# First cross attention of a Perceiver block: scores by key kept in SBUF, their maxima taken by key and turned

## The chip, the cores and the metric

The kernel runs on one core of one Trainium2 chip. The engines of a core work side by side, each through its own queue in order: TensorE (PE, matrix products; its weight loads are shown as PEld), VectorE (DVE), ScalarE (ACT), GpSimd (POOL) and SyncE (SP, which here only issues transfers). They meet through semaphores. Products land in PSUM, the other operands lie in SBUF. The metric is the device time of one execution in microseconds, the median of several runs.

## The reference, cut to what matters

The whole computation is a chain of twelve blocks (attention, feed-forward and expert layers) on `x` of shape (16, 64, 256), four of which attend to a context of shape (16, 1601, 256). The change touches the first of them alone. Its weights are `w_q, w_k, w_v, w_o` (256 x 256). As the kernel computes it, with 16 heads of 16 columns, for each batch `b`:

```python
h = layernorm(x)
q, k, v = h @ w_q, ctx @ w_k, ctx @ w_v           # heads of 16 columns
s = einsum('qd,kd->qk', q[head], k[head])         # 64 x 1601 for each of 16 heads
s = where((s == 0) & (key <= query), finfo.min, s)   # zeros at and below the diagonal do not count
p = softmax(s / 4)
x = x + concat(p @ v[head]) @ w_o
```

All of it is in fp32. The softmax subtracts the true maximum over the 1601 keys for each query and head.

## The kernel before

The keys of a batch are cut into 13 chunks of 128 (the last has 65 valid rows), so there are 16 x 13 = 208 chunks. The 256 columns are two groups `g` of 128; a group holds four blocks of 32 rows, and a block holds two heads. `x.qb` keeps each query twice, once with the columns of the even heads and once with those of the odd ones (zeros elsewhere, `own2`), so that one product over 32 rows gives two heads side by side in 128 columns (2 heads x 64 queries). Four such products, one for each block, run beside each other on the array; so do four products with 32 weight columns each (`columns`).

`stream` (L2507) writes TensorE's whole order out by hand: with `self.pinned` every matmul issued by `mm` and `tr` keeps the order of the program. One step `k` handles two chunks:

1. `weights` (L335) makes the scores of the chunk pair of the next step in the four-bank PSUM tile `sc` (tag `w`, one buffer): `scores_by_key` (L2447) gives keys on the partitions; then products of `minus` and `x.rows` subtract the maxima inside PSUM, in bf16 parts, and products of `x.z` with `never` put a huge negative value where a score was zero at or below the diagonal. ScalarE's exponential (L361) reads the tile into `e`.
2. `project` (L2515) makes the next piece of keys (`kT`) or values (`v`) of a later batch in a PSUM tile `pk` (tag `bk`, two buffers), which ScalarE copies out (L286). Each batch has 13 pieces: six of keys, one with the last chunk of both, six of values.
3. `values` (L2553) multiplies the exponentials by the values into `acc`; GpSimd adds the exponentials up over the chunks into `tot` (L2551), from which `finish_heads` (L2418) makes the sums with products of ones.
4. The jobs of `extra` (L395) make the maxima for a batch ahead of its weights: `maxima` (L288) makes all scores of a batch a second time, by query, in the same PSUM tile `w`; VectorE reduces 2048 columns at a time (L299); `last_maxima` (L301) handles the last chunk, joins the parts and splits the result into three bf16 parts; `max_rows` (L324) turns them into rows.

`load` (L267) fetches a batch's context with two transfers on SP's queue and makes `qb` on GpSimd; for the second batch it also calls `gate_biases` (L1139), which prepares a bias of a later stage. `out` (L398) makes the output product of two batches (128 rows), adds it to `x` and, at the last rows, begins the next stage (`start`, `norm`, `turned`). The pool `weights` (`w8`, L114, three buffers of 8 KB a partition) belongs to no stage: in this one the next stage's large weights are already fetched into it (L118). `awake` (L2632) issues products whose result nobody reads.

Of the kernel before, what the change touches and what calls it, by code (L numbers as in the profile page):

```python
# [20 lines left out]
P = 128  # L21
# [43 lines left out]
class Sections:  # L65
# [157 lines left out]
    def l0_xattn(self):  # L223
# [6 lines left out]
        with ExitStack() as ctx:  # L230
            sb = ctx.enter_context(tc.tile_pool(name="l0x", bufs=1, reuse_waits="tile"))
            sb2 = ctx.enter_context(tc.tile_pool(name="l0x2", bufs=2, reuse_waits="tile"))
            ps = ctx.enter_context(tc.tile_pool(name="l0x_ps", bufs=2, space=PSUM, reuse_waits="tile"))
            wq = self.w2(d["L0_xattn_w_q"], "wq")
# [4 lines left out]
            xln = sb2.tile([P, NT, D], F32, tag="e", name="xln", bufs=3)  # L239
            xT = sb.tile([P, KC, T], F32, tag="xT", name="xT")  # L240
            qT = sb.tile([P, KC, T], F32, tag="qT", name="qT")
            identb = sb.tile([P, P], BF16, tag="identb", name="identb")
            nc.vector.tensor_copy(identb, self.ident)
            minus = sb.tile([P, P], BF16, tag="minus", name="minus")
            nc.gpsimd.memset(minus, -1.0)
            never = sb.tile([P, P], BF16, tag="never", name="never")
            nc.vector.tensor_scalar(never, self.ident, NEVER, None, ALU.mult)
            parts = sb.tile([P, 4, 32], BF16, tag="parts", name="parts")
            nc.gpsimd.memset(parts, 0.0)
# [9 lines left out]
            own = self.c("own2")  # L259
            tril = self.c("tril2").unsqueeze(1).to_broadcast([P, 4, S])  # L260
            ones = self.c("ones")[:, :32]

            def quad():

                return ps.tile([P, 4, 512], F32, tag="w", name="sc", bufs=1)

            def load(b):  # L267
                if b == 1:
                    self.gate_biases(sb2)
                x = Streamed(b)  # L270
# [3 lines left out]
                x.v = sb2.tile([P, NCH, D], F32, tag="v", name="v")  # L274

                x.qb = sb2.tile([P, 2, 2, S], F32, tag="qb", name="qb", bufs=3)
                nc.gpsimd.tensor_tensor(
# [3 lines left out]
                x.m4 = sb2.tile([P, 2, 4, 4], F32, tag="m4", name="m4")  # L281
                x.z = sb2.tile([P, 2, 4, S], BF16, tag="z", name="z", bufs=3)
                return x

            def copy(out, in_):
                nc.scalar.copy(out, in_)  # L286

            def maxima(x, g, i):  # L288


                pm = quad()
                for r in range(4):
                    o = slice(32 * r, 32 * r + 32)
                    self.mm(
                        pm[:, r, :], x.qb[o, g].rearrange("p h s -> p (h s)"), x.kT[i][o, g, :512], start=True, stop=True)
                if i == 0:
                    nc.vector.scalar_tensor_tensor(x.z[:, g], pm[:, :, :S], 0.0, tril, ALU.is_equal, ALU.mult)
                    nc.vector.scalar_tensor_tensor(pm[:, :, :S], x.z[:, g], NEVER, pm[:, :, :S], ALU.mult, ALU.add)
                nc.vector.tensor_reduce(x.m4[:, g, :, i], pm, AX.X, ALU.max)  # L299

            def last_maxima(x):  # L301


                w = SK - 1536
                pm = quad()
                for g in range(2):
                    for r in range(4):
                        o = slice(32 * r, 32 * r + 32)
                        self.mm(
                            pm[:, r, g * P : g * P + w], x.qb[o, g].rearrange("p h s -> p (h s)"),  # L310
                            x.kT[2][o, g, 512 : 512 + w], start=(g == 0), stop=True, skip_group_check=True,
                        )
                nc.vector.tensor_reduce(
# [4 lines left out]
                for s in range(3):  # L318
                    to = parts[:, :, 2 * s : 2 * s + 2]
                    nc.vector.tensor_copy(to, m)  # L320
                    if s < 2:
                        nc.vector.tensor_tensor(m, m, to, ALU.subtract)
# [12 lines left out]
            def weights(pair):  # L335

                pm = quad()
                if pair[0][0].b == pair[0][1] == 0:
                    self.awake(ps, 2, "acc")
# [2669 lines left out]
```

## Time and profile before

| what | value |
|---|---|
| median of 3 runs | 3684.61 us (3680.84 to 3687.91) |
| the profiled execution, its own time | 3680.2 us |
| its span, first to last instruction | 3678.4 us |
| mean granted clock of TensorE | 0.984 |
| first product of the keys of this stage (L2622, tile `pk`) | 20.6 us |
| last output of its heads (L2436) | begins at 851.9 us |
| ScalarE copying keys and values (L286), 128x512 | 585 to 586 ns |
| GpSimd adding exponentials (L2551), 128x1024 | 2363 ns between 100 and 700 us |

A row of a group reads: line, engine, operation, output <- inputs, shapes, count | busy time, mean ns of one | idle time of the engine just before, and what ended it. In a timeline a row reads: start, length, engine, line, operation, names, shapes, count, and in brackets the idle time before. One line stands for all products that helpers issue: L2622 is inside `mm`, so products are told apart by their tiles. A matmul in fp32 leaves two records, one in bf16 leaves one.

### The profile page before, as it was taken

How to read it: one execution, taken by the hardware profiler on the slowest of the kernel's cores; microseconds unless marked ns; L12 is line 12 of the kernel's file. 1: busy time of each engine (PE TensorE's matmuls, PEld its weight loads, DVE VectorE, ACT ScalarE, POOL GpSimd, SP SyncE). 2: the span in 40 equal slices, each digit the busy share in tenths (PEclk: the TensorE clock that was granted, in tenths of full speed). 3: DMA queues.
4: the chain of work that ended last, by engine and by line, in shares of the span. 5: the costliest groups of instructions: out<-in, count | busy, mean ns of one | idle time of the engine just before them, and what ended most of it. 6: DMA issues, size and time to landing. Idle time of an engine off the chain costs nothing.

```text
span 3678.4 us, 87682 instructions
## 1 busy us (share of the span) xinstructions
PE 3444.5 (94%) x39417; PEld 2061.5 (56%) x39432; DVE 1974.8 (54%) x3645; ACT 1457.2 (40%) x2093; POOL 1290.7 (35%) x784
## 2 busy tenths in 40 slices
PE   9999999998999989999987988999999889999997
PEld 3555555454665665555555666556666555555554
DVE  5344333446555646656656555577777765333446
ACT  2333333343444424444433443466666612111124
POOL 1555555562101123333322100577777630000002
PEclk9999999999999989999999999999999999999999
DMA  4111001101333355342101000211111004111550
GB/s 148 39 39 39 29 31 39 39 8 55 98 91 99 121 168 168 121 149 105 45 27 41 1 6 22 94 58 40 53 45 40 9 5 177 40 38 33 242 220 13
DMA packets 108135, 260.82 MB, mean 71 GB/s; under 512 B 9609, under 2 KB 76172, under 8 KB 105456
## 3 DMA queue, kind: packets, MB, share of 16 engines
q1 hardware_dynamic: 99040, 223.14, 17.1%
q10 hardware_dynamic: 6912, 27.27, 2.4%
q8 instruction: 309, 5.06, 0.6%
q0 software_dynamic: 1808, 4.80, 0.4%
q14 instruction: 66, 0.54, 0.0%
HBM read 248.85 MB, written 6.33 MB: 69 GB/s over the span
## 4 chain that ended last, share of the span: by engine, by line
PE 73%; DVE 14%; ACT 8%; issue 3%; DMA 1%; POOL 0%; SPq 0%; ACTq 0%; DVEq 0%; POOLq 0%
PE sc L2622 15%; PE pk L2622 14%; PE lin L2622 6%; ACT e L361 5%; PE lin_t L2622 5%; PE acc L2622 5%; PE pu L2622 4%; PE gate L2169 3%; PE up L2169 3%; PE lin L216 3%; PE pc L1789 3%; PE prz L2622 2%; DVE m L299 2%; PE gelu_t L1703 2%; PE turn L2640 1%
## 5 line engine op out<-in xcount | busy, mean ns | idle before, releaser
L2551 POOL TENSOR_TENSOR tot<-tot,e 128x1024 f32<-128x1024 f32 (+1 forms) x340 | 807.1, 2374 | 349.6 <-ACT e L361 237.3
L299 DVE TENSOR_REDUCE m<-sc 128x4 f32<-128x2048 f32 x96 | 220.1, 2293 | 267.6 <-PE sc L2622 266.5
L1932 DVE SCALAR_TENSOR_TENSOR e<-sc,row_L_xattn_nbias,free 128x2048 f32<-128x2048 f32 x104 | 244.3, 2349 | 104.9 <-PE sc L2622 101.2
L1934 ACT ACTIVATE e<-e 128x2048 f32<-128x2048 f32 x104 | 198.6, 1910 | 232.5 <-DVE e L1932 232.5
L2622 PE MATMUL sc<-qb,kT 32*128 32x128 f32 x6656 | 245.0, 284 | 47.6 <-DVE e L1932 17.8
L361 ACT ACTIVATE e<-sc 128x2048 f32<-128x2048 f32 x104 | 195.2, 1877 | 224.2 <-PE sc L2622 222.6
L2622 PEld LDWEIGHTS sc<-qb,kT 32*128 32x128 f32 x6656 | 206.1, 187 | 92.8 <-issue 24.8
L2622 PEld LDWEIGHTS acc<-e,v 128*32 128x32 f32 x6656 | 189.1, 110 | 75.9 <-issue 50.6
L2622 PE MATMUL acc<-e,v 128*32 128x128 f32 x6656 | 221.4, 273 | 5.1 <-ACT e L1935 5.1
L2622 PE MATMUL pk<-cT,wk 128*32 128x512 f32 (+1 forms) x2048 | 205.4, 519 | 4.5 <-ACT kT L286 4.5
L2622 PE MATMUL pk<-wv,cT 128*32 128x256 f32 x3328 | 203.4, 382 | 0.0
L1935 ACT ACTIVATE e<-e 128x2048 f32<-128x2048 f32 x104 | 198.8, 1912 | 3.2
L2622 PE MATMUL pk<-wkv,cT 128*32 128x256 f32 x3328 | 193.5, 381 | 0.0
L2622 PE MATMUL pk<-cT,wkv 128*32 128x512 f32 (+1 forms) x2048 | 192.5, 515 | 0.0
L2622 PE MATMUL sc<-kT,qb 32*128 32x512 f32 (+2 forms) x1536 | 140.2, 460 | 23.3 <-ACT e L361 18.6
L2622 PEld LDWEIGHTS pk<-wv,cT 128*32 128x32 f32 x3328 | 97.7, 110 | 112.3 <-issue 57.4
L2173 ACT ACTIVATE g<-gate 128x512 f32<-128x512 f32 x68 | 40.6, 597 | 293.3 <-PE gate L2169 293.3
L1789 PE MATMUL pc<-ew,eh 128*128 128x256 f32 x640 | 156.7, 388 | 0.0
L1322 POOL TENSOR_TENSOR e<-e,mx 128x512 f32<-128x512 f32 x96 | 81.8, 883 | 193.1 <-DVE mx L1321 193.1
L2174 DVE TENSOR_TENSOR hT<-up,g 128x512 f32<-128x512 f32 x68 | 47.0, 691 | 182.3 <-PE up L2169 178.6
L2210 POOL TENSOR_TENSOR x<-x,row_L_xattn_bv 128x1024 f32<-128x1024 f32 x2 | 4.7, 2346 | 396.6 <-DVE xln L158 396.6
L2622 PE MATMUL pu<-cn,e 128*64 128x257 f32 (+1 forms) x1248 | 141.6, 382 | 1.6 <-POOL e L1332 1.5
(544 smaller groups left out, 6468.0 us busy)
## 6 DMA issues: line engine op xcount, KB each, us to landing
cT<-in_ctx_t SPq DMA_DIRECT2D x128, 832.0 KB, 6.2
cn<-in_ctx_n SPq DMA_DIRECT2D x32, 1664.0 KB, 12.0
piece<-in_ctx_n ACTq DMA_DIRECT2D x32, 640.0 KB, 4.0
w<-in_L_attn_W SPq DMA_DIRECT2D x8, 1024.0 KB, 6.5
piece<-in_ctx_n ACTq DMA_DIRECT2D x16, 384.0 KB, 3.7
w<-in_L_ffn_W SPq DMA_DIRECT2D x16, 256.0 KB, 2.9
down<-in_L_ffn_w_down SPq DMA_DIRECT2D x16, 256.0 KB, 2.8
gate<-in_L_ffn_w_gate SPq DMA_DIRECT2D x16, 256.0 KB, 2.8
```

The lines of the kernel that those rows point to most:

```text
L216: nc.tensor.matmul(pm, xT[:, k, t * P : (t + 1) * P], w[:, k, :], start=(k == 0), stop=(k == kc - 1))
L299: nc.vector.tensor_reduce(x.m4[:, g, :, i], pm, AX.X, ALU.max)
L361: nc.scalar.activation(e, pm, AF.Exp, scale=0.25)
L1322: pin(nc.gpsimd.tensor_tensor(p.e, p.e, p.mx.unsqueeze(2).to_broadcast(p.shape), ALU.subtract))
L1703: nc.tensor.matmul(pm, w[:, c, lo : lo + m], cT[:, c, :], start=(c == 0), stop=(c == nk - 1))
L1789: nc.tensor.matmul(pc[:, n, j, :], s.eh[i][:, c, tok], ew2[:, c, cols], start=False, stop=(c == 3))
L1932: nc.vector.scalar_tensor_tensor(e16, pm16, nb, free[:, at : at + P].unsqueeze(1).to_broadcast([P, 16, P]), ALU.add, ALU.mult)
L1934: nc.scalar.activation(e, e, AF.Relu)
L1935: nc.scalar.activation(e, e, AF.Square)
L2169: nc.tensor.matmul(pm[-1], w[:, k, n * P : (n + 1) * P], xT[:, k, tok], start=(k == 0), stop=(k == KC - 1))
L2551: nc.gpsimd.tensor_tensor(tot[:w], x.first if c == 1 else tot[:w], e[:w], ALU.add)
L2622: ins = self.nc.tensor.matmul(*args, **kw)
```

## The change

The products by query are gone. A unit is now one batch and one group `g` (32 units); the order runs over quads, four chunks of 13 x 32 = 416, so 104 quads and five more rounds to drain (`LAG`).

- A quad's scores are made once, by key, in the PSUM tile `w` (still one buffer of four banks). `hide` puts in the masked zeros on VectorE for the first chunk of a unit. ScalarE copies the four banks to an SBUF tile `raw`; VectorE takes the running maximum of each chunk into `top` of the unit (128 keys' places x 4 blocks x 128).
- After a unit's last chunk `turn_maxima` turns `top` by products with the identity, VectorE reduces over the places, `spread_maxima` turns the result back so that every partition has the row of maxima, and ScalarE copies it to `mx`.
- `lower` subtracts `mx` from the raw scores on GpSimd (on VectorE for the last four quads); ScalarE then makes the exponential in place, in SBUF.
- The values are kept with a column of ones for each pair of heads (16 + 1 columns a head, interleaved by a strided copy on VectorE), so that the products of the values also give the sums; each head has its own product of 64 columns. `finish` joins the halves, moves the sums with products of `pair_sum`, and scales.
- Seven buffers hold the raw scores: four of this stage, three in `w8`. The copies of the keys stay on ScalarE, those of the values go to VectorE. VectorE, ScalarE and GpSimd are written in order too (`Written`).
- A further constant, `heads`, is fetched on SP's queue, and `gate_biases` is called before the loop, ahead of the first `load`.

```diff
+            V, A, G = (Written(tc, e) for e in (nc.vector, nc.scalar, nc.gpsimd))
...
+            heads = sb.tile([P, 3, P], F32, tag="heads", name="heads")
+            nc.sync.dma_start(heads, d["heads"].rearrange("p (k n) -> p k n", n=P))
...
+            vs = [sb.tile([P, NCH, H // 2, 2, 17], F32, tag=f"v{i}", name="v") for i in range(2)]
+            for v in vs:
+                nc.gpsimd.memset(v, 1.0)
...
+            self.gate_biases(
+                [sb2.tile([32, 2, 4 * D], F32, tag="raw", name="bias_raw", bufs=4)[:, i] for i in range(2)],
+                sb2.tile([32, 4 * D], BF16, tag="kT", name="part", bufs=5))
+
+            UNITS, LAG, LEAD = 2 * B, 5, 4
+            Q = UNITS * NCH // 4
...
+            order = [(keys, 0, 0), "v", (keys, 0, 1), "v", (keys, 0, 2), (last_keys,), "v", (keys, 1, 0), "v",
+                     (keys, 1, 1), "v", (keys, 1, 2), "v"]
+            LATE = 2
...
+            def scores(q):
+
+                pm = ps.tile([P, 4, 4, P], F32, tag="w", name="sc", bufs=1)
+                for i in range(4):
+                    b, g, c = of(4 * q + i)
+                    x = xs[b]
+                    kT, at = (x.kT[g, c // 4], c % 4 * P) if c < 12 else (x.last[:, g], 0)
                     for r in range(4):
                         o = slice(32 * r, 32 * r + 32)
                         self.mm(
+                            pm[:, r, i, :], kT[o, at : at + P], x.qb[o, g].rearrange("p h s -> p (h s)"),
+                            start=(i == 0), stop=True, skip_group_check=True)
+                return pm
+
+            def hide(q, pm):
+
+                for i in range(4):
+                    if (4 * q + i) % NCH == 0:
+                        shape = [S, 4, P]
+                        of = pm[:S, :, i, :]
+                        z = sb2.tile(shape, BF16, tag="z", name="z")
+                        V.scalar_tensor_tensor(
+                            z, of, 0.0, upto[:S].unsqueeze(1).to_broadcast(shape), ALU.is_equal, ALU.mult)
+                        V.scalar_tensor_tensor(of, z, NEVER, of, ALU.mult, ALU.add)
+
+            def maxima(q, pm):
+
+                for i in range(4):
+                    n = 4 * q + i
+                    u, c = divmod(n, NCH)
+                    if c == 0:
+                        us[u] = Streamed(u)
+                        us[u].top = sb2.tile([P, 4, P], F32, tag="top", name="top")
+                        V.tensor_copy(us[u].top, pm[:, :, i, :])
+                        continue
+                    w = min(P, SK - c * P)
+                    top = us[u].top[:w]
+                    V.tensor_tensor(top, top, pm[:w, :, i, :], ALU.max)
...
+            def keep_values(x, pm, cs):
+                V.tensor_copy(
+                    x.v[:, cs[0] : cs[0] + len(cs), :, :, :16],
+                    pm[:, : len(cs) * D].rearrange("p (j a h e) -> p j a h e", h=2, e=16, a=H // 2))
...
+            def turn_maxima(u):
+
+                pt = ps.tile([P, 4, P], F32, tag="bk", name="mt")
                 for r in range(4):
+                    for j in range(4):
+                        o = slice(32 * j, 32 * j + 32)
+                        self.mm(pt[o, r, :], us[u].top[:, r, o], self.ident, start=(r == 0), stop=True, skip_group_check=True)
+                us[u].m = sb2.tile([P, 4], F32, tag="m", name="m")
+                V.tensor_reduce(us[u].m, pt, AX.X, ALU.max)
+
+            def spread_maxima(u):
+
+                pt = ps.tile([P, 4, P], F32, tag="bk", name="mx")
+                for r in range(4):
+                    self.tr(pt[:, r, :], us[u].m[:, r : r + 1].to_broadcast([P, P]), self.ident)
+                us[u].mx = sb2.tile([P, 4, P], F32, tag="mx", name="mx", bufs=3)
+                us[u].pt = pt
+
+            def lower(q, E):
...
+                    E.tensor_tensor(part, part, us[u].mx.unsqueeze(2).to_broadcast([P, 4, to - n, P]), ALU.subtract)
...
+            def values(q):
...
+                    pairs = xs[b].v.rearrange("p c a h e -> p c a (h e)")
+                    for h in range(2):
+                        for j in range(4):
+                            self.mm(
+                                u.acc[32 * j : 32 * j + 32, h * S : (h + 1) * S], pairs[:w, c, 4 * g + j, h : h + 32],
+                                e[:w, j, i, h * S : (h + 1) * S], start=(c == 0 and h == 0), stop=(c == NCH - 1),
+                                skip_group_check=True)
...
+            def take(u):
+                us[u].sums = sb2.tile([P, P], F32, tag="sums", name="sums")
+                A.copy(us[u].sums, us[u].acc[:, :P])
+
+            def finish(u):
+                x = us.pop(u)
+                acc = x.acc
+                for h in range(2):
+                    for j in range(4):
+                        o = slice(32 * j, 32 * j + 32)
+                        self.mm(acc[o, 2 * S : 3 * S], pair_sum[:, h, o], x.sums[:, h * S : (h + 1) * S],
+                                start=(h == 0), stop=(h == 1), skip_group_check=True)
+                both = sb2.tile([P, S], F32, tag="both", name="both")
+                V.tensor_scalar(both, acc[:, :S], own[:, 0:1], None, ALU.mult)
+                V.scalar_tensor_tensor(both, acc[:, S : 2 * S], own[:, 1:2], both, ALU.mult, ALU.add)
+                V.reciprocal(acc[:, 3 * S : 4 * S], acc[:, 2 * S : 3 * S])
+                b, g = divmod(u, 2)
+                V.tensor_tensor(hT[:, g, b * S : (b + 1) * S], both, acc[:, 3 * S : 4 * S], ALU.mult)
...
+            for q in range(-(LEAD // 2), Q + LAG):
+                new, old = 0 <= q < Q, 0 <= q - LAG < Q
+                for u in ends(q - 1):
+                    A.copy(us[u].mx, us[u].pt)
+                closed = ends(q - 1 - LAG)
+                for u in closed:
+                    take(u)
+                if 0 <= q - LAG + 1 < Q:
+                    lower(q - LAG + 1, G if q < Q else V)
+                if new:
+                    pm = scores(q)
+                if old:
+                    A.activation(raws[q - LAG], raws[q - LAG], AF.Exp, scale=0.25)
+                if new:
+                    hide(q, pm)
+                    if q % 7 < 3:
+                        raws[q] = self.wp.tile([P, 4, 512], F32, tag="w8", name="raw", bufs=3)
+                    else:
+                        raws[q] = sb2.tile([P, 4, 512], F32, tag="raw", name="raw", bufs=4)
+                    raws[q] = raws[q].rearrange("p r (i n) -> p r i n", n=P)
+                    A.copy(raws[q], pm)
+                    maxima(q, pm)
+                piece(2 * q + LEAD)
+                for u in closed:
+                    finish(u)
+                piece(2 * q + LEAD + 1)
+                for u in ends(q):
+                    turn_maxima(u)
+                if 0 <= q - Q + 7 < NT - 1:
+                    out(q - Q + 7)
+                if old:
+                    values(q - LAG)
+                for u in ends(q):
+                    spread_maxima(u)
+            take(UNITS - 1)
+            finish(UNITS - 1)
+            self.awake(ps, 3, "bk")
+            out(NT - 1)
```

## The prediction

> **What bounds the kernel now.** I read the page first (busy shares, the chain that ended last), then the groups by shape from 100 to 700 us, where the first cross attention runs undisturbed, then its timeline, then rows of other stages that have the shapes of the new instructions.
>
> ```profile
> PE 3444.5 (94%) x39417; PEld 2061.5 (56%) x39432; DVE 1974.8 (54%) x3645; ACT 1457.2 (40%) x2093; POOL 1290.7 (35%) x784
> PE 73%; DVE 14%; ACT 8%; issue 3%; DMA 1%; POOL 0%; SPq 0%; ACTq 0%; DVEq 0%; POOLq 0%
> ```
>
> TensorE is busy 94% of the span and 73% of the chain. In the stage, by group:
>
> ```profile
> L299 DVE TENSOR_REDUCE m<-sc 128x4 f32<-128x2048 f32 x72 | 165.1, 2293 | 204.7 <-PE sc L2622 203.9
> L361 ACT ACTIVATE e<-sc 128x2048 f32<-128x2048 f32 x77 | 144.5, 1877 | 172.5 <-PE sc L2622 172.5
> L2622 PE MATMUL sc<-kT,qb 32*128 32x512 f32 x572 | 81.6, 639 | 15.3 <-ACT e L361 15.3
> L2622 PE MATMUL sc<-rows,minus 32*128 32x512 bf16 x284 | 28.7, 374 | 0.0
> ```
>
> 72 reductions, six a batch, are 12 batches. VectorE and ScalarE wait for TensorE (204.7 and 172.5 us); it hardly waits for them. The timeline gives durations and the pace:
>
> ```profile
> 205.50 0.18 DVE L317 TENSOR_REDUCE m<-m 128x8 f32<-128x32 f32 x1
> 205.52 1.17 PE L2622 MATMUL sc<-qb,kT 32*128 32x128 f32 x32 [0.82 <-DVE m L313]
> 206.51 0.39 PE L2622 MATMUL sc<-rows,minus 32*128 32x512 bf16 x4
> 206.84 1.92 PE L2622 MATMUL pk<-cT,wk 128*32 128x512 f32 x16
> ...
> 711.11 0.19 DVE L317 TENSOR_REDUCE m<-m 128x8 f32<-128x32 f32 x1
> ```
>
> Ten batches lie between the two L317: 50.56 us each, 101.1 for two. The stage's first product starts at 20.6 us and its last output ends at 852.1: 831 us, of which 16 batches at this pace are 809 and 22 lie at the ends.
>
> **TensorE's share of the change.** Removed per batch, busy time of the groups over 12: the maxima's products 81.6 and 8.1 us (6.8 + 0.7), `rows` 2.6, `never` 0.6, the sums from `tot` 0.6, the turned parts 0.2, and 3 us of waits: about 14.5. Added per batch: two turns of the maxima (32 records each, like a 32-record `acc` burst, 1.06 us), two spreads (8 transposing records, 1.04 us by the row of L182), 0.45 for the head sums: 4.6. The values take twice as many matmuls of half the width; a burst of this very shape stands in a later stage:
>
> ```profile
> 3001.16 1.10 PE L2622 MATMUL acc<-qp,kv 128*32 128x64 f32 x64
> ```
>
> 64 records (an fp32 matmul leaves two) are one quad (four chunks of 128 keys), 0.9 us until the next can start: per batch 5.9 us against 7.0 before. If TensorE still set the pace, some 10 us a batch, 145 to 175 us, would go.
>
> **What takes its place.** A quad's scores now leave PSUM twice: ScalarE copies the tile (L361's shape, 1.85 us) and VectorE takes maxima of it, four operations of 128x512. PSUM tile `w` has one buffer, so the next quad's scores, next in TensorE's written order, wait for both. Do both read at once? L1796 and L1797 tell: ScalarE and VectorE read the same PSUM tile into different tiles, and no data passes between them, yet:
>
> ```profile
> L1797 DVE TENSOR_SCALAR rb<-pc x24: 680/690/693, 1994.5 to 2259.3; 128x512 f32<-128x512 f32 x24
> ...
>   ACT sp L1796: 32.7, 10
> ```
>
> VectorE waited ten times, 32.7 us, for ScalarE's reading to end. In the first transposes it is the other way round: ScalarE's reading starts 0.03 us after VectorE's ends, four times of four. So I take the readings as one after the other, copy before maxima, as written; each maxima operation touches all four banks of the copy, so none can start early. The Trainium skill speaks on both sides. PSUM — Partial Sum Buffer, section Specifications (TRN2), gives ScalarE and VectorE full bandwidth in parallel, as long as banks do not collide; by that the time would be the first rival's below. Its section PSUM bank collisions raise a hardware error counts two engines reading one bank and the same 32 partitions as such a collision; by that it is my forecast.
>
> A maxima operation reads one PSUM and one SBUF operand: 691 ns by L2174 (128x512, same operands). A dependent VectorE operation starts 0.03 after the one before. Loop of a plain quad: scores 1.17, hand-over 0.07, copy 1.85, 0.03, maxima 4 x 0.69 + 3 x 0.03 = 2.87, back to TensorE 0.06: **6.05 us**. TensorE's own work in it: 0.99 + two projections of 1.74 + 0.90 = 5.37. Loop, not TensorE, sets the pace.
>
> Thirteen quads are two batches and hold four unit ends (a unit is one batch and 128 of its 256 columns):
> - Five plain: 30.6 (one is 6.4, `take` and the exponential being late).
> - Three after a unit's end: ScalarE copies the spread maxima (0.59) and does the exponential (1.91) before its copy, which starts at 2.5 instead of 1.2: 7.3 each, 22.0.
> - One of these with `hide` first (64x512, 0.69 and 0.70): 7.5.
> - Four ends. The turn needs the finished maxima and a `bk` bank. With `hide` the copy ends at 4.6, maxima at 7.4; if the first projection was of values, its bank is read out by VectorE after them, 8.1. Turn 1.06, reduction 0.69, spread 0.87 to TensorE's next: 11.1 with a late start of VectorE, twice. With keys first the turn starts at 6.8, but 1.2 of finishing stands before the reduction: 10.6. Without `hide` 9.6. Sum 42.4.
>
> Total 102.5 against 101.1: +1.4 per two batches, **+11 us** over eight. Ends: 3.5 of first projections; first maxima wait some 6 for the ten gate-bias operations (VectorE until 31 us; they stood before the first maxima already); after the last quad subtractions on VectorE (2048 elements, 2.29 by L1802's 1223 ns for 1024), exponentials and finish, 16; three for the last output products. 29 against 22: **+7**.
>
> **The clock.** In the two longest ends TensorE stands idle 3.6 us before the turn. Windows (length, then busy time of PE, PEld, DVE, ACT, POOL with counts, granted clock, DMA share, GB/s) show what such a pause does:
>
> ```profile
> 34.00:38.00 4.00, 3.56 (x20) 0.91 (x24) 2.30 (x2) 0.00 (x0) 0.00 (x0) 0.62 0.26 84
> ...
> 2921.00:2925.00 4.00, 4.00 (x40) 2.95 (x44) 2.66 (x4) 3.70 (x2) 0.19 (x3) 0.50 0.00 0
> ```
>
> The first follows 2.98 us without a matmul, the second 4.14: the granted clock is 0.62 and 0.50 over four us, and the 32 score records at 2920.9 take 2.09 instead of 1.17. 0.62 is 3 us at half speed, so 1.5 us lost. For 16 such ends that is 24 us; nothing, if all of it falls into the loop's slack. Turn, values and spread (2.8 us) directly follow the pause and lie on the path, so I take three quarters: **+18**.
>
> **Work off the path.** GpSimd subtracts 2048 elements a quad: 2.30 ns each by L2551, 4.7 us, against 7.9 a quad on average; by L1322 (883 ns for 512) 3.5. It stays hidden up to 7.9. It loses the sums (`tot`). Its two fills with ones (3536 columns; 0.95 us for 1024) end by 10 us, before its first use at 19.8. ScalarE: 1.85 + 1.91 + 0.9 a quad, hidden but for the cases above. SP's queue gets the `heads` load (196 KB) and the gate biases ahead of the first context: some 1.6 us, while that landed long before its use at 20.6. Three `w8` buffers hold scores until the stage's end, so two 1 MB weight loads move from 23.7 us to there; first use is 58 us after it (910.2), landing 6.5: covered; uncovered 7 to 13 us.
>
> **Sum.** Profiled execution 3680.2 (span 3678.4 and 1.8 around it) + 11 + 7 + 18 = 3716; the median shown is 4.4 above that execution: **3721**. The same walk laid over the old order gives 98.1 for two batches where the trace has 101.1, 3% short; as much here is +25.
>
> **Rivals.** One, faster: both engines do read at once. The loop is 1.17 + 0.07 + 2.87 + 0.06 = 4.2, under TensorE's 5.37; ends wait 1 to 2 us; two batches take 82.4, so 8 x 18.7 = 150 us go, the ends give back 5: **3540**. It decides if the first maxima start within 0.2 us of the scores' end. For it: nothing passes between the two readers; against it, the 32.7 us above. Chance 0.11. Two, no slower: the walk is 3% too long (25) because late exponentials and read-outs overlap better than a strict order says, and the clock stays up (18): **3678**. For it: the pauses of 0.8 us before scores in 205.5 to 711.1 us left the granted clock at 1.00; against it, the walk was short, not long, on the old order. 0.24, of which 0.14 faster and 0.10 the same. Three: GpSimd's subtraction and VectorE's maxima exclude each other: 4.7 + 2.9 and 1.3 of other VectorE work are 8.9 a quad, 104 x 1.0 more than 7.9: **3825**. For it: L2436 (two SBUF inputs) takes 1232 ns under GpSimd's sums and 293 without; against it, L428 (one input in PSUM, like the maxima) took 418 with GpSimd busy. 0.05. My forecast has 0.60.
>
> **From these.** The range goes down to 3655 (the second rival without the 7 at the ends and another 2% of the walk, 16) and up to 3765 (25 as on the old order, 6 to the clock's full 24, 13 for uncovered weights). A measurement of this kernel tells some 0.2%, 7 us, from no change. Faster 0.14 + 0.11 = 0.25, same 0.10, slower 0.60 + 0.05.
>
> **What would show it.** Maxima starting 0.03 us after the raw copy, TensorE waiting for VectorE's maxima before scores (0.6 us in plain quads) and before turns (2 to 4 us); 51 us between the ends of batches; GpSimd without waits on VectorE; values near 0.9 a quad; long records after the turns' waits. Maxima beginning with the copy prove me wrong at once; an even pace of 41 us a batch too.

## The result and the profile after

The changed kernel takes 3715.17 us (median of 3711.39 to 3716.35), the kernel before 3684.51 beside it: a ratio of 1.0082, interval 1.0064 to 1.0099. It is slower, by 30.7 us; 3721 was forecast. The profiled execution is one of 3715.3 us, its span 3713.5 against 3678.4, the mean granted clock 0.972 against 0.984.

The page's busy times and its chain by engine:

```profile
PE 3370.3 (91%) x42270; PEld 2086.1 (56%) x42270; DVE 2103.7 (57%) x4048; ACT 1608.6 (43%) x2149; POOL 1315.9 (35%) x721
PE 65%; DVE 21%; ACT 9%; issue 4%; POOL 0%; DMA 0%; another core or an unknown queue 0%; SPq 0%; ACTq 0%; DVEq 0%; POOLq 0%
```

TensorE's busy time fell by 74 us (3444.5 to 3370.3), and yet the span grew by 35: TensorE now waits. VectorE's share of the chain rose from 14% to 21%. The groups between 100 and 750 us name the partners:

```profile
L59 POOL TENSOR_TENSOR raw<-raw,mx 128x2048 f32<-128x2048 f32 x65 | 296.6, 4594 | 89.2 <-ACT mx L59 89.2
L59 DVE TENSOR_TENSOR top<-top,sc 128x512 f32<-128x512 f32 x285 | 195.8, 687 | 241.5 <-ACT raw L59 234.1
...
L59 ACT COPY raw<-sc 128x2048 f32<-128x2048 f32 x84 | 156.6, 1864 | 83.0 <-PE sc L2739 45.4 <-DVE sc L59 36.8
...
L2739 PE MATMUL sc<-qb,kT 32*128 32x128 f32 x2488 | 95.6, 284 | 54.7 <-DVE top L59 53.2 <-ACT raw L59 1.5
```

Read upwards from the last row: TensorE's scores wait for VectorE's maxima (53.2 us), the maxima wait for ScalarE's copy (234.1), the copy for the scores or for `hide`: a ring of three. GpSimd's subtraction, with 4.59 us the longest operation here, waits only for `mx`; nobody's row names it as the releaser. (L2739 is now the line in `mm`, L59 the one in `Written`.)

The timeline of two quads, the first after a unit's end, the second plain:

```profile
460.03 1.17 PE L2739 MATMUL sc<-qb,kT 32*128 32x128 f32 x32
...
460.62 1.92 ACT L59 ACTIVATE raw<-raw 128x2048 f32<-128x2048 f32 x1
...
462.43 1.86 ACT L59 COPY raw<-sc 128x2048 f32<-128x2048 f32 x1
...
464.32 2.85 DVE L59 TENSOR_TENSOR top<-top,sc 128x512 f32<-128x512 f32 x4 [4.93 <-ACT raw L59]
...
467.32 1.17 PE L2739 MATMUL sc<-qb,kT 32*128 32x128 f32 x32 [1.64 <-DVE top L59]
...
468.61 1.87 ACT L59 COPY raw<-sc 128x2048 f32<-128x2048 f32 x1 [0.79 <-PE sc L2739]
...
470.50 2.85 DVE L59 TENSOR_TENSOR top<-top,sc 128x512 f32<-128x512 f32 x4 [2.73 <-ACT raw L59]
```

In the plain quad the copy starts 1.29 us after the scores did, the maxima 0.02 after the copy's end, and 0.16 after the maxima the next scores start, at 473.51: 6.19 us. In the one before, `mx` and the exponential hold the copy up until 462.43, and the quad takes 7.29.

Where do the 30.7 us lie? From the first scores, at 25.9 us in both kernels, 91 quads (14 batches) take 705.1 us; at the old pace of 50.56 a batch they took 707.8. The loop itself is a draw, 2.7 us better. The last 13 quads and what follows, up to the next stage's first `lin_t` (869.2 us in the kernel before, 894.7 now), take 163.7 us against 135.5: +28.2. The stage as a whole gives +25.5. The rest of the span, +9 to 10 in the profiled execution, comes up in stages whose instructions did not change; it is looked at with the experiments.

### The profile page after: what moved, and what is told of

The parts are those of the page before. It is cut to its first block, busy times and chain, and to the rows that moved or that the text cites. A ratio compares the mean times of both kernels' runs of the same rounds, so it can differ in the third digit from the quotient of the medians.

```text
span 3713.5 us, 93831 instructions
## 1 busy us (share of the span) xinstructions
PE 3370.3 (91%) x42270; PEld 2086.1 (56%) x42270; DVE 2103.7 (57%) x4048; ACT 1608.6 (43%) x2149; POOL 1315.9 (35%) x721
## 4 chain that ended last, share of the span: by engine, by line
PE 65%; DVE 21%; ACT 9%; issue 4%; POOL 0%; DMA 0%; another core or an unknown queue 0%; SPq 0%; ACTq 0%; DVEq 0%; POOLq 0%
PE pk L2739 11%; PE sc L2739 10%; DVE top L59 7%; PE lin L2739 7%; ACT raw L59 5%; PE lin_t L2739 5%; PE pu L2739 4%; PE acc L2739 3%; PE gate L2286 3%; PE up L2286 3%; PE lin L216 3%; PE pc L1906 3%; PE prz L2739 2%; PE turn L2757 2%; PE gelu_t L1820 2%
## 5 line engine op out<-in xcount | busy, mean ns | idle before, releaser
L59 POOL TENSOR_TENSOR raw<-raw,mx 128x2048 f32<-128x2048 f32 (+3 forms) x123 | 460.0, 3772 | 342.4 <-ACT mx L59 342.4
L2668 POOL TENSOR_TENSOR tot<-tot,e 128x1024 f32<-128x1024 f32 (+1 forms) x170 | 405.7, 2387 | 105.8 <-ACT e L2052 78.9
L59 DVE TENSOR_TENSOR top<-top,sc 128x512 f32<-128x512 f32 (+1 forms) x384 | 263.8, 687 | 314.8 <-ACT raw L59 304.9
L2739 PE MATMUL sc<-qb,kT 32*128 32x128 f32 x6400 | 244.1, 286 | 81.1 <-DVE top L59 63.5
L2739 PEld LDWEIGHTS sc<-qb,kT 32*128 32x128 f32 x6400 | 205.1, 189 | 120.4 <-ACT raw L59 40.8
L59 ACT COPY raw<-sc 128x2048 f32<-128x2048 f32 x104 | 193.8, 1864 | 116.6 <-PE sc L2739 62.1
L2739 PE MATMUL pk<-wv,cT 128*32 128x256 f32 x3328 | 212.0, 394 | 0.1
L2739 PE MATMUL pk<-cT,wk 128*32 128x512 f32 (+1 forms) x2048 | 202.1, 516 | 0.0
L59 ACT ACTIVATE raw<-raw 128x2048 f32<-128x2048 f32 x104 | 199.3, 1918 | 1.7 <-POOL raw L59 0.9
L2739 PE MATMUL pk<-wkv,cT 128*32 128x256 f32 x3328 | 193.5, 381 | 0.0
L2739 PE MATMUL pk<-cT,wkv 128*32 128x512 f32 (+1 forms) x2048 | 192.5, 514 | 0.0
L2739 PEld LDWEIGHTS pk<-wv,cT 128*32 128x32 f32 x3328 | 104.8, 113 | 83.2 <-issue 27.7
L2739 PE MATMUL sc<-cT,qT 128*64 128x512 f32 (+1 forms) x768 | 142.1, 520 | 4.7 <-ACT scs L1419 4.2
L2739 PE MATMUL pu<-cn,e 128*64 128x257 f32 (+1 forms) x1248 | 141.2, 381 | 2.0 <-POOL e L1449 2.0
```

Of the source, the lines that this page charges most:

```text
L59: ins = getattr(self.engine, name)(*args, **kw)
L2668: nc.gpsimd.tensor_tensor(tot[:w], x.first if c == 1 else tot[:w], e[:w], ALU.add)
L2739: ins = self.nc.tensor.matmul(*args, **kw)
```

## The experiments

The theory under test: **the two readings of the one PSUM tile stand in a row, copy before maxima, and this ring sets the loop; what is late at its end (the turn, the next copy) makes the long quads**. Against it: TensorE's own work or clock, VectorE and GpSimd holding each other up, GpSimd's subtraction, the stage's end. "13 quads" is a cycle of two batches, 99.7 us in the changed kernel's undisturbed cycles.

**x1: maxima from the copy in SBUF.**

```diff
-                    maxima(q, pm)
+                    maxima(q, raws[q])
```

> VectorE takes the maxima from ScalarE's copy in SBUF, not from the PSUM tile; result unchanged. Theory (the two readings of the one PSUM tile stand in a row and set the pace): the tile is free when the copy ends, 1.17 + 0.07 + 1.85 + 0.06 = 3.2 us after the scores began, under TensorE's own 5.4, so plain quads fall from 6.18 to about 5.4, quads after a unit's end from 7.3 to about 5.8, ends stay near 9.7 (the turn still waits for the maxima); 13 quads 88 instead of 99.7, the kernel about 3625. Rival A (with both operands in SBUF, VectorE's maxima and GpSimd's subtraction hold each other up): maxima of 1.2 us each instead of 0.69, subtractions well over 4.7, ends 2 us longer, 13 quads 96 to 110, the kernel 3690 to 3800. Rival B (TensorE's own work or its clock sets the pace): 13 quads stay at 99.7, the kernel at 3715.

Measured: 3991.95 us, ratio to before 1.0844 (1.0822 to 1.0865); 13 quads 139. The PSUM tile is free early, as meant: quads come down to 5.6 where VectorE runs freely. But VectorE does not. Two views of one place in its timeline, VectorE's and GpSimd's:

```profile
294.28 2.80 DVE L59 COPY top<-raw 128x512 f32<-128x512 f32 x1 [2.01 <-ACT raw L59]
297.12 4.92 DVE L59 TENSOR_TENSOR top<-top,raw 128x512 f32<-128x512 f32 x1
...
292.22 9.27 POOL L59 TENSOR_TENSOR raw<-raw,mx 128x2048 f32<-128x2048 f32 x2
```

A maxima operation of 0.69 us takes 4.92 while GpSimd subtracts; 84 of 416 operations on `top` took over 1.5 us, the longest 11.9. So rival A is real, and far stronger than the 1.2 us expected from a row of the trace before. The Trainium skill has the rule (SBUF — State Buffer, section Who interferes with whom): a VectorE operation with two inputs in SBUF and a GpSimd operation that reads SBUF exclude each other, for a whole instruction at a time. This run agrees, with 4.92 for 0.69; in the changed kernel, where one of the inputs lies in PSUM, 285 maxima average 687 ns beside the same subtractions.

**x8: x1 without the subtraction**, to tell that from slow operands.

```diff
-                    E.tensor_tensor(part, part, us[u].mx.unsqueeze(2).to_broadcast([P, 4, to - n, P]), ALU.subtract)
```

> x1 (maxima from the copy in SBUF) with the subtraction of the maxima left out as in x4, so that GpSimd is all but idle. Theory (x1's maxima of 1.5 us mean, up to 2.9, come from VectorE and GpSimd holding each other up where both have all operands in SBUF): maxima fall to 0.7 us or less, GpSimd's few other operations stay, plain quads about 5.4, ends about 9; 13 quads 83 to 90 instead of x1's 139, the kernel about 3610. Rival (a VectorE operation with two operands in SBUF is slow by itself, or the copy's late end sets the pace): maxima stay above 1.2 us, 13 quads above 120, the kernel above 3850.

Measured: 3655.13 us, ratio 0.9927 (0.9901 to 0.9954); 13 quads 93 to 98, more than expected, since the turn at a unit's end still waits for copy and maxima (55.2 us for VectorE's maxima between 100 and 690 us). The group of the maxima from 100 to 690 us:

```profile
L59 DVE TENSOR_TENSOR top<-top,raw 128x512 f32<-128x512 f32 x275 | 190.3, 692 | 197.4 <-ACT raw L59 190.4
```

692 ns with GpSimd quiet, 1496 in x1. The mutual exclusion is shown. With the maxima in SBUF most plain quads are 5.58 to 5.80, near the 5.4 that was estimated for TensorE's own work: that they were 6.19 was due to the PSUM tile.

**x2 and x5: the tile in halves.** Both split the scores into two PSUM tiles of two banks. They differ in the order in which four readings are written. x2:

```diff
-                    A.copy(raws[q], pm)
-                    maxima(q, pm)
+                    A.copy(raws[q][:, :2], pm[0])
+                    A.copy(raws[q][:, 2:], pm[1])
+                    maxima(q, pm[1], slice(2, 4))
+                    maxima(q, pm[0], slice(0, 2))
```

> The scores of a quad lie in two PSUM tiles of two banks; ScalarE copies half one, then half two, VectorE takes the maxima of half two first, then of half one; result unchanged, VectorE has 8 operations of 128x256 a quad for 4 of 128x512. Theory (readings in a row): the engines read different halves at once; both are read 1.17 + 0.07 + about 3.1 = 4.3 us after the scores began, under TensorE's 5.4; plain quads 5.4 instead of 6.18, the turn at an end hardly waits (8.3 instead of 9.7), after an end about 6.3 instead of 7.3; 13 quads about 86 instead of 99.7, the kernel about 3605. If copy and maxima of different banks do not run at once either, or TensorE's own work sets the pace: 13 quads stay at 99 to 103, the kernel at 3715 or above.

Measured: 3799.07 us, ratio 1.0316 (1.0299 to 1.0334); 13 quads 112.6. The expectation failed, and the timeline says how:

```profile
345.96 1.93 ACT L59 COPY raw<-sc 128x1024 f32<-128x1024 f32 x2 [2.34 <-PE sc L2743]
...
347.92 3.48 DVE L59 TENSOR_TENSOR top<-top,sc 128x256 f32<-128x256 f32 x8 [2.48 <-ACT raw L59]
```

VectorE starts after both copies, since its first four operations read the half that is copied second, and the copy of that half is written ahead of them. The reading written first goes first; separate banks alone gain nothing. x5 exchanges two lines:

```diff
                     A.copy(raws[q][:, :2], pm[0])
-                    A.copy(raws[q][:, 2:], pm[1])
                     maxima(q, pm[1], slice(2, 4))
+                    A.copy(raws[q][:, 2:], pm[1])
                     maxima(q, pm[0], slice(0, 2))
```

(`hide` does half one first as well.)

> As x2_halves, with two lines exchanged: the order written is copy of half one, maxima of half two, copy of half two, maxima of half one (x2 had both copies written ahead of both maxima, and its VectorE began only after the second copy, although no bank was shared). Result unchanged. Theory (a reading of a PSUM tile waits for the reading of the same tile written before it by the other engine, and for nothing else): maxima of half two start within 0.2 us of the scores' end, beside the copy of half one; both halves are read 1.17 + 0.07 + 8 x 0.435 = 4.7 us after the scores began, under TensorE's 5.4; plain quads 5.4 instead of after's 6.18, after an end about 5.9 instead of 7.3, ends 8.3 or (with hide) 10; 13 quads about 87 instead of 99.7, the kernel about 3613. Rival A (the two engines never read PSUM at once): maxima start after a copy, 13 quads about 112 as in x2, the kernel near 3799. Rival B (TensorE's work sets the pace): 13 quads 97 to 100, the kernel 3700 to 3715.

Measured: **3599.2 us, ratio 0.9767 (0.9752 to 0.9782)**; 13 quads 86.5, 87 expected. This beats both kernels.

```profile
342.69 1.01 ACT L59 COPY raw<-sc 128x1024 f32<-128x1024 f32 x1 [0.45 <-PE sc L2743]
342.70 3.48 DVE L59 TENSOR_TENSOR top<-top,sc 128x256 f32<-128x256 f32 x8 [0.70 <-PE sc L2743]
...
344.58 1.01 ACT L59 COPY raw<-sc 128x1024 f32<-128x1024 f32 x1 [0.87 <-PE pk L2743]
```

Copy and maxima start 0.01 us apart, on different banks, and neither takes longer for it: a half's copy averages 1013 ns here and 1016 in x2, where they stand in a row, a maxima operation 420 in both. Plain quads are 5.58 to 6.17, after an end 5.58 to 5.92 instead of 7.29 to 7.66, ends 7.95 to 9.40 instead of 9.24 to 10.58. Rivals A and B fall: it was neither PSUM as a whole nor TensorE's work, but two readings of the same banks, one after the other.

**x12: the smallest test**, the two lines of the changed kernel exchanged, one tile as before.

```diff
-                    A.copy(raws[q], pm)
                     maxima(q, pm)
+                    A.copy(raws[q], pm)
```

> The changed kernel with two lines exchanged: VectorE's maxima of a quad are written ahead of ScalarE's copy of it; tile and banks as they are. Result unchanged. Theory (the two readings stand in the order written; what the copy delays is only the next quad's scores, what the maxima delay is also the turn at a unit's end): maxima start 0.07 after the scores, the copy 0.03 after the maxima; plain quads stay at 6.1 to 6.2; after an end 6.2 to 6.4 instead of 7.3, since the copy no longer starts behind mx and exponential; ends 8 to 10 instead of 9.2 to 10.6, where the copy of keys behind the copy of scores frees the bank late; 13 quads 90 to 94 instead of 99.7, the kernel 3640 to 3670. Rival (the sum of both readings is all that counts): 13 quads stay at 98 to 100, the kernel 3700 to 3715.

Measured: 3654.65 us, ratio 0.9926 (0.9913 to 0.9939); 13 quads 92.7.

```profile
344.80 2.85 DVE L59 TENSOR_TENSOR top<-top,sc 128x512 f32<-128x512 f32 x4 [2.67 <-PE sc L2739]
...
347.76 1.87 ACT L59 COPY raw<-sc 128x2048 f32<-128x2048 f32 x1 [1.79 <-DVE top L59]
```

Now ScalarE waits for VectorE (1.79 us), the mirror image of the changed kernel. The sum of the two readings is what it was, and plain quads stay at 6.12; but three of the four quads after an end fall from 7.29 to 6.13, because `mx` and the exponential now fit beside the maxima, and three of four ends from 9.2 to 9.7 down to 8.67. The fourth falls less, from 10.58 to 10.04, and that in four of seven cycles only; in the other three it takes 11.3 to 11.6. Its turn waits as long in both cases, but what follows differs, as in these two cycles:

```profile
284.29 1.08 PE L2739 MATMUL mt<-cst,top 128*32 128x128 f32 x32 [2.52 <-DVE v L59]
...
378.11 1.94 PE L2739 MATMUL mt<-cst,top 128*32 128x128 f32 x32 [2.52 <-DVE v L59]
```

In the three long ones the values behind the turn run at about half speed (1.90 to 1.95 us instead of 1.08). The place of one line is worth 56 to 60 us, by the second and the first measurement of the changed kernel (x11); 55 of them lie in the stage, whose successor's first `lin_t` starts at 839.5 instead of 894.7 us.

**x3: ScalarE's copy ahead of the exponential.**

```diff
-                if old:
-                    A.activation(raws[q - LAG], raws[q - LAG], AF.Exp, scale=0.25)
                 if new:
                     hide(q, pm)
...
                     maxima(q, pm)
+                if old:
+                    A.activation(raws[q - LAG], raws[q - LAG], AF.Exp, scale=0.25)
```

> ScalarE copies a quad's scores before it does the exponential of the earlier quad, not after; result unchanged. Theory (the copy starts late after a unit's end, since mx copy and exponential stand ahead of it): quads after an end fall from 7.3 to about 6.2, plain ones stay at 6.18, the values may wait 0.4 us for their exponential, inside TensorE's idle time; 13 quads about 95.5 instead of 99.7, the kernel about 3683. Rival: the late exponential holds up the values and with them the spread of the maxima; 13 quads stay near 99.7 or rise, the kernel 3715 or above.

Measured: 3698.36 us, ratio 1.0046 (1.0029 to 1.0063), half of the gain expected; 13 quads 98.9. In its trace the next stage's first `lin_t` starts at 887.7 us, only 7 before the changed kernel's; the rest of the 17 us between the medians does not lie in this stage. Three of the four quads after an end are 6.2 to 6.3, about as expected; three of the four ends took much of it back, 9.94, 11.5 and 11.0 instead of 9.71, 9.71 and 10.58. Groups of 100 to 750 us:

```profile
L2739 PE MATMUL acc<-raw,v 128*32 128x64 f32 x5024 | 100.7, 235 | 18.4 <-ACT raw L59 17.9
...
L2739 PE MATMUL mt<-cst,top 128*32 128x128 f32 x832 | 33.4, 309 | 54.6 <-ACT kT L59 46.1 <-DVE top L59 8.4
```

The turn (`mt`) now waits for ScalarE's copy of the keys, 46.1 us, which stands behind the exponential; it needs that bank. The values wait for the exponential, 17.9.

**x6: x5 and x3 together.** The edits are those two.

> x5 and, in addition, ScalarE copies the scores before the exponential of the earlier quad, as in x3. Result unchanged. Theory: quads after an end fall to 5.5, but ends lose up to 1 us as in x3, since the copies of keys stand behind the exponential; 13 quads 85 to 88, the kernel 3600 to 3620. If the copies of keys behind the exponential hold up TensorE's banks now that the loop is shorter: 13 quads above 90, slower than x5.

Measured: 3755.87 us, ratio 1.0197 (1.0176 to 1.0218); 13 quads about 107. The exchange that had gained a little in x3 lost 157 us against x5. From 100 to 850 us:

```profile
L2743 PE MATMUL acc<-raw,v 128*32 128x64 f32 x5376 | 109.0, 237 | 75.0 <-ACT raw L59 75.0
...
L2743 PE MATMUL mt<-cst,top 128*32 128x128 f32 x896 | 34.3, 300 | 61.6 <-ACT kT L59 32.2 <-DVE v L59 29.4
```

The second half's copy waits for VectorE, the exponential for that copy, the values for the exponential (75.0 us): plain quads 7.05. My expectation had added the parts without laying ScalarE's queue out once more. In x5 ScalarE works at the exponential while it would otherwise wait.

**x4: no subtraction in the changed kernel.** The edit is that of x8.

> Leaves out the subtraction of the maxima, GpSimd's in the loop and VectorE's in the last quads; maxima, turns and spreads are still made. Theory (GpSimd's subtraction is off the path): 13 quads stay within 1 us of 99.7; only the last quads gain, four or five subtractions of 2.3 us and the wait for the spread maxima, some 10 to 12 us, the kernel about 3704. Rival (GpSimd's work slows VectorE or ScalarE, or late subtractions hold the exponentials): 13 quads fall by 3 us or more, the kernel below 3685.

Measured: 3700.21 us, ratio 1.0052 (1.0032 to 1.0072). Undisturbed cycles stay at 99.6 to 99.7: GpSimd's subtraction costs the loop nothing. From the last scores' start to the next stage's first `lin_t` it is 50.7 instead of 51.9, the twelve quads before 106.6 instead of 111.9: some 6.5 us where 10 to 12 were expected. The median lies 15 us under the changed kernel's, of which the stage explains some 4 (that `lin_t` starts at 891.0 against 894.7 us); the rest is in the later stages, see x11.

**x7: TensorE kept awake at the stage's end.**

```diff
+                if q == Q - 1:
+                    self.awake(ps, 5, "bk")
                 for u in ends(q):
                     turn_maxima(u)
...
+                if q >= Q:
+                    self.awake(ps, 2 if q == Q else 1, "bk")
                 if old:
                     values(q - LAG)
```

> The changed kernel with idle products on TensorE at the stage's end: five (128x512) ahead of the last turn of the maxima, two and then one a round ahead of the last values. Result unchanged. Theory (after the last scores TensorE's pauses let its clock fall to about half, and its work there lies on the chain): the last turn falls from 1.94 to about 1.1 us, the last lin from 2.08 to 1.1, values from 1.8 to 2.4 down to 1.1, the three idle products after the last finish from 4.7 to 1.8; together some 8 us, 13 quads unchanged, the kernel about 3707. Rival (VectorE's subtractions and ScalarE's exponentials alone set the end): the records are shorter, but the stage ends less than 2 us earlier, the kernel at 3713 or above.

Measured: 3709.55 us (3703.65 to 3716.09), ratio 1.0071 (1.0055 to 1.0086). The windows at the stage's end (length, busy time of PE, PEld, DVE, ACT, POOL with counts, granted clock, DMA share, GB/s), of the changed kernel and of x7:

```profile
843.00:875.00 32.00, 19.82 (x507) 15.51 (x508) 15.76 (x25) 15.01 (x11) 0.48 (x4) 0.71 0.26 84
```

```profile
843.00:872.00 29.00, 24.53 (x554) 14.31 (x544) 16.03 (x26) 15.38 (x12) 0.48 (x4) 1.00 0.28 93
```

The granted clock is 0.71 there, and 1.00 with the idle products. The timelines show the last turn, a `lin` and the idle products at the end, first in the changed kernel, then in x7:

```profile
850.80 1.94 PE L2739 MATMUL mt<-cst,top 128*32 128x128 f32 x32 [6.43 <-DVE top L59]
...
852.66 2.08 PE L2739 MATMUL lin<-wo,xT 128*128 128x256 f32 x4
...
872.84 4.70 PE L2739 MATMUL awake<-cst 128*128 128x512 f32 x6
```

```profile
851.10 1.08 PE L2743 MATMUL mt<-cst,top 128*32 128x128 f32 x32 [1.84 <-DVE top L59]
...
852.11 1.13 PE L2743 MATMUL lin<-wo,xT 128*128 128x256 f32 x4
...
869.87 2.84 PE L2743 MATMUL awake<-cst 128*128 128x512 f32 x6
```

After a pause of 6.43 us the turn ran at about half speed; with idle products in the pause it did not. The way from the last scores to the next stage is 5.3 us shorter in the trace, 8 were expected. In the medians, 5.6 apart with overlapping runs, this alone would not be shown.

**x9 and x10: x5 with that, and with the gate biases later.** x10 does VectorE's ten operations for the gate biases behind the maxima of the first three quads:

```diff
                     maxima(q, pm[0], slice(0, 2))
+                    if q < 3:
+                        next(gate)
```

> x5 and x7 together: halves read in turns, and idle products on TensorE at the stage's end. Result unchanged. Theory (the two act at different places and add): 13 quads 86.5 as in x5, the stage's end 5 us earlier; the kernel about 3594. Rival (with the shorter loop the idle products come late or the clock never falls at the end): same as x5, 3599 or above.

> x9, and the ten gate-bias operations of VectorE, which stand among the read-outs of the queries before the first product, are done three at a time behind the maxima of the first three quads. Result unchanged. Theory (they hold up the read-outs of qT and the first hide): the first product starts 1.5 to 2 us earlier against the loads' end, the first maxima no longer wait 1.2 us behind them; the stage ends some 2 us earlier, the kernel about 3592, which these rounds may not tell from x9. Rival (3.2 us more of VectorE in each of the first three quads hold up the next scores): the first three quads 2 us longer each, the kernel 2 to 4 us above x9.

Measured: x9 3597.99 us (3586.45 to 3607.39), ratio 0.9777 (0.9757 to 0.9798); x10 3599.43, ratio 0.9785 (0.9762 to 0.9808). In the medians neither can be told from x5. The traces show 1.9 of the 5 us that x9 should gain: from the last scores' start to the first `lin_t` it is 46.7 us against 48.6 in x5, with a granted clock of 0.95 instead of 0.73 in the first 32 us, though x9 loses 1.89 us there in a pause inside the values that waits for nothing the trace shows. In x10 the first 13 quads take 95.4 us against 87.0 in x9, which speaks for its rival: that work stood better where the change had put it.

**x11: the changed kernel once more.** No edit.

> The changed kernel itself, nothing edited, profiled a second time. In its first profile the stages behind the changed one (from the first product with hT to the end) took 2819 us against 2809 before and 2806 to 2814 in the other kernels, though their instructions are the same. If that belongs to this program: again about 2818 behind the stage, the kernel 3715. If it is one execution's chance: 2805 to 2814, the kernel 3703 to 3712.

Measured: 3710.58 us (3701.29 to 3718.38), ratio 1.0067 (1.0054 to 1.0079). From the next stage's first `lin_t` to the end this execution took 2815 us, the first one 2819, the kernel before 2809; over all kernels here it was 2802 (x9) to 2819. The extra comes in jumps, at places that differ: one in the chain of waits of the first profile, which the chains of x4 and x11 don't have, is

```profile
1406.29 6.14 another core or an unknown queue
```

The trace can't name what ended it. The instructions there are the same in all. So the split is not firm. The stage costs 25.5 us in the first profile and 29.5 in the second, the stages behind it 9.6 and 6.1, and the second execution lies 5 us above its median; the medians put the whole at 30.7 and, here, at 25.4. That the stage is slower stands in both; how much the untouched stages add, and why, stays open. Part of such differences is visible: in x11, TensorE pauses for 1.94 us in the middle of a quad's scores (until 132.24 us), and the trace names nothing that it waits for.

## Why the prediction was right, and where it was wrong

The forecast's time, 3721, lies 6 us from the median, and its mechanism holds. But its terms do not add up the way they were put; errors of some 30 us in both directions offset each other, so that the sum came this close is in good part luck.

- **The readings in a row: right.** The maxima start 0.02 to 0.03 us after the copy; plain quads are 6.19 (6.05 predicted), quads after an end 7.29 (7.3), the one with `hide` 7.66 (7.5). x12 against the changed kernel and x5 against x2 show the cause, since in each pair only the order on the reading engines differs. x5 also shows what rival one would have been worth: 86.5 for 13 quads where it had 82.4.
- **The ends: 39.2 us instead of 42.4.** Predicted 11.1, 11.1, 10.6 and 9.6, measured 9.71, 9.71, 10.58 and 9.24. The step that failed is "The turn needs the finished maxima": it needs those of its own unit. At an end the other chunks of the quad belong to the next unit, and their maxima run beside the turn:

```profile
455.46 0.68 DVE L59 TENSOR_TENSOR top<-top,sc 65x512 f32<-65x512 f32 x1 [2.01 <-ACT raw L59]
456.07 0.68 DVE L59 COPY top<-sc 128x512 f32<-128x512 f32 x1
456.30 1.08 PE L2739 MATMUL mt<-cst,top 128*32 128x128 f32 x32 [1.22 <-DVE top L59]
456.78 1.41 DVE L59 TENSOR_TENSOR top<-top,sc 128x512 f32<-128x512 f32 x2
```

 The last chunk of the unit (65 rows) is done at 456.1; the turn follows, while VectorE has three more operations to do. So two batches take 99.7 and not 102.5, and the +11 of eight of them became about -11.
- **The clock: +18 in the wrong place.** Pauses before the turn are 1.2 to 1.9 us in the loop, not 3.6, and from 100 to 750 us the granted clock is 0.99. The 91 quads lie only 7 us above seven undisturbed cycles (705.1 against 697.9): 3.1 in the first cycle, and 4.1 in two others, in quads like 7.27 and 7.49 that stand where others have 6.19. There TensorE's projections run at about half speed, behind a pause of 1.6 or 2.0 us (granted clock 0.86 from 360 to 372 us, 0.87 from 330 to 343):

```profile
335.78 1.17 PE L2739 MATMUL sc<-qb,kT 32*128 32x128 f32 x32 [2.00 <-DVE top L59]
336.88 3.27 PE L2739 MATMUL pk<-wv,cT 128*32 128x256 f32 x32
...
344.15 1.93 PE L2739 MATMUL pk<-wv,cT 128*32 128x256 f32 x32
```

 Of the 34 pauses over 1.5 us between 100 and 731 us, most left the speed as it was. The clock fell most where the term did not look, in the stage's last 145 us: 0.84 to 0.94 from 731 to 843 us, 0.71 from 843 to 875.
- **The ends of the stage: +7 predicted, +28 measured behind the 91st quad, clock included.** 31.5 us run from the last scores to the last `finish`, where 9.6 and 16 were laid out; x7 puts 5 of them down to the clock. The larger omission, read from the trace and not tested by a run, is the output products of the last quads. They take turns at the `bk` banks, which VectorE reads out behind its maxima. Groups of 745 to 843 us:

```profile
L2739 PE MATMUL lin<-wo,xT 128*128 128x256 f32 x24 | 9.6, 539 | 10.9 <-DVE v L59 8.3 <-ACT kT L59 2.6
```

 10.9 us of waits in six products. After one of them `lin`, values and scores run at half speed (2.07, 1.94 and 2.09 us instead of 1.13, 1.10 and 1.17). The twelve last quads take 111.9 instead of some 90. The walk had counted output products only after the last quad.
- **GpSimd: right.** 4.59 us a subtraction, with no wait of the loop on it; x4 leaves it out and the cycles stay. What was argued against rival three, the mutual exclusion of GpSimd and VectorE, was right: with one input in PSUM the maxima stay at 687 ns. x1 shows the exclusion as soon as that input moves to SBUF.
- **Values: right**, 1.08 to 1.10 us for 64 records. (A spread of the maxima is four records and 0.65 us, where the sum had eight and 1.04; it changes nothing above.) Of the 20 us that TensorE was to save per two batches, x5 shows 14.6 (101.1 to 86.5); its ends still wait for banks.
- **The weight loads moved to the stage's end cost nothing**, as taken: issued at 861.6 us, and the product that first needs them starts at 935.4 instead of 910.2 us, 25.2 later, while the next stage's first product (`lin` with `wkv`) is 25.0 later.
- **The gate biases** cost less than feared: the first scores start at 25.9 us in both kernels, and the first `hide` 1.3 us after their end, where the first maxima were to wait some 6.

## What to carry to other kernels

When two engines read the same PSUM tile, write down which reading comes first in the program, and what waits behind each: the readings add up, and the one that is needed for the longer chain belongs first. Better, give each engine its own banks and let them change places; but the order written must then alternate as well, or the split costs more than it brings (x2 against x5: 200 us for the place of one line, with `hide` turned to match). And after any such reordering lay out each engine's queue anew: a move that gained 7 us of this stage alone (x3) lost 157 in the faster version (x6).

## What the runs showed of the hardware that was not expected

- ScalarE and VectorE read different PSUM banks at once without slowing down (x5: 1013 and 420 ns an operation; x2, in a row: 1016 and 420). The Trainium skill (PSUM — Partial Sum Buffer, section Specifications (TRN2)) says so too, as long as banks do not collide. Its section PSUM bank collisions raise a hardware error counts readings of one bank and the same partitions as a collision; what would happen then no run here shows.
- The exclusion between VectorE and GpSimd is worse than one instruction for one: of the 84 long operations of x1, three lasted some 12 us, one of them from 260.97 to 272.85, across three GpSimd subtractions that follow each other without a pause and end at 264.5, 268.9 and 272.3. A plain copy from SBUF to SBUF is held up as well (2.80 us for 0.42).
- VectorE's half operations are not half as long: 420 ns for 128x256 against 687 for 128x512, so a quad's maxima cost 3.48 instead of 2.85. x5 gains in spite of that.
